# The maxima in the attention heads of a four-layer network: GpSimd subtracts them in every second block, VectorE builds their diagonal matrix

## The chip, the cores and the metric

The kernel runs on one core of a Trainium2 chip. The time is the device time of one execution in microseconds, the median over runs. In the profile TensorE is PE (its weight loads PEld), VectorE is DVE, ScalarE is ACT, GpSimd is POOL, and SyncE, which issues most DMAs, is SP. Everything is float32.

## The reference

Four residual layers act on four images of 32 x 32 pixels with 384 channels. The change lies in layer 0, a deformable attention with six heads of 64 channels:

```python
q = jnp.einsum('bhwc,cd->bhwd', x, w_q) + b_q
...
xs = _bilinear_sample(xg, pos)              # keys and values at learned positions
k = (xs @ w_k + b_k).reshape(Bq, n, HEADS, HC)
v = (xs @ w_v + b_v).reshape(Bq, n, HEADS, HC)
attn = jnp.einsum('bmhc,bnhc->bhmn', qh, k) * scale
bias = _bilinear_sample(rpe_img, disp)      # a bias for each pair of query and key
...
attn = jax.nn.softmax(attn + bias, axis=-1)
out = jnp.einsum('bhmn,bnhc->bmhc', attn, v).reshape(Bq, Hq, Wq, NC)
return out @ w_out + b_out
```

Here n = 1024 pixels, so that each head has 1024 x 1024 logits. Layer 1 is another attention with 12 heads, layer 2 a ratio of box sums, layer 3 a local attention over 3 x 3 windows. A group norm stands before each layer.

## The kernel before, in words

**Front and trunk.** The layer 0 of an image is its front, the layers 1 to 3 are its trunk. The front of image 0 runs alone at the start, through a hand-ordered pipeline of its own (`heads0`, which the diff does not touch). After that the trunk of image b runs together with the front of image b + 1. Both are Python generators that yield weights of their work; `Net.layer3` steps the trunk and, whenever the front has fallen behind its share, the front. Instructions are thus emitted interleaved. The framework then orders each engine's instructions when the program is built, by its own estimates and the dependencies, except where a call pins them. So on the chip each engine has a fixed queue, and a change of one instruction's engine can move others by a few places.

**One half-head** (`head0(h, q)`): one head and half of the queries, 512 of them. There are 12 in an image and 36 in images 1 to 3. Keys lie on the partitions, 128 to a block, in eight blocks j; queries lie along the free axis.

- For each block, GpSimd issues an indirect DMA (L944) that gathers a window of bias rows into `win` (four buffers). ScalarE and VectorE interpolate it in two steps, in `z` (L956, L957) and in `lg` (L961, L962; 13 buffers). TensorE multiplies keys by queries (L968), VectorE adds the product to `lg` (L971) and keeps a running maximum `rmax` (L973, L975).
- Then the maximum over all keys must be had for each query and brought to all partitions. TensorE transposes `rmax` in four squares (L982), VectorE reduces them to `top`, 128 x 4 (L986). GpSimd makes `diag`, four diagonal matrices 128 x 128 with these maxima, out of the identity (L988). TensorE multiplies a matrix of ones by `diag` (L990), so that every partition holds every query's maximum, and ScalarE copies it out of PSUM to `tb`, 128 x 512 (L994).
- Then, block by block, VectorE subtracts `tb` from `lg` in place (L1001), ScalarE takes the exponential in place (L1002), and TensorE adds the block's product with the values to one PSUM bank, `po` (L1003). Each float32 matmul shows as two in the profile. ScalarE copies the result (L1007) and the row of sums (L1016) out.

**What runs beside it.** The trunk's largest stage is layer 1 (`pair`), two heads at a time, eight blocks of keys for each pair. For each block, GpSimd scales the group similarities into `sg` (L1682, two buffers); TensorE makes the logits in `big` (L1699; `big` is a PSUM tile of two banks, with two buffers), ScalarE takes the exponential to `e` (L1707); TensorE makes the group weights out of `sg` (L1729) or by transposing kept ones (L1724), in PSUM `bank` (four buffers); VectorE multiplies `e` by them and sums (L1736); ScalarE keeps a copy for later blocks (L1741); TensorE multiplies by the values (L1671, after VectorE's L1662 to L1665). In between, `sums_step` prepares the next pair: TensorE's scores (L1561) in `big`, VectorE's maxima (L1570), ScalarE's exponentials with sums (L1574). At the end of an image's trunk come layers 2 and 3; there GpSimd adds a tile of 128 x 1024 (L1892).

The methods that the diff touches, and what calls them:

Of the kernel before, what the change touches and what calls it, by code (L numbers as in the profile page):

```python
# [21 lines left out]
ALU = mybir.AluOpType  # L22
# [4 lines left out]
P = 128  # L27
# [39 lines left out]
def bc(ap, axis, n):  # L67

    u = ap.unsqueeze(axis)
    shape = list(u.shape)  # L70
    shape[axis] = n
    return u.broadcast_to(shape)
# [357 lines left out]
class Front(Lane):  # L430
# [500 lines left out]
    def head0(self, h, q):  # L931

        nc, v = self.nc, self.nc.vector
        f = self.f
        k, r0 = h // 2, (h % 2) * GC
        rows = slice(r0, r0 + GC)
        HH, HN = HW // 2, N // 2
        queries = self.qpad[rows, k, 1 + HH * q : 1 + HH * (q + 1), 1 : 1 + HW]
        logits = []
        rmax = self.wt([P, HN], "rmax", 2)  # L940
        for j in range(NJ):
            c = j * G + h
            win = self.wt([P, (HH + 1) * WROW], "win", 4)
            nc.gpsimd.indirect_dma_start(  # L944
                out=win,
                out_offset=None,
                in_=self.strips[:, :],
                in_offset=bass.IndirectOffsetOnAxis(
                    ap=self.widx[:, q, c : c + 1], axis=0
                ),  # L950
            )
            wv = win.rearrange("p (r c) -> p r c", c=WROW)
            sc = lambda i, t: f[:, i, t, c : c + 1]

            z = self.wt([P, HH, HW + 1], "z", 3)
            nc.scalar.activation(z, wv[:, 0:HH, 0 : HW + 1], AF.Copy, scale=sc(1, 1))  # L956
            v.scalar_tensor_tensor(  # L957
                z, wv[:, 1 : HH + 1, 0 : HW + 1], sc(0, 1), z, ALU.mult, ALU.add
            )
            lg = self.wt([P, HH, HW], "lg", 13)  # L960
            nc.scalar.activation(lg, z[:, :, 0:HW], AF.Copy, scale=sc(1, 0))  # L961
            v.scalar_tensor_tensor(lg, z[:, :, 1 : HW + 1], sc(0, 0), lg, ALU.mult, ALU.add)  # L962
            logits.append(lg.rearrange("p y x -> p (y x)"))
            if j % 2:
                ps = [self.bank() for _ in range(2)]
                for u in range(2):
                    w, mov = self.logits_of(h, q, j - 1 + u)
                    nc.tensor.matmul(ps[u], w, mov, start=True, stop=True)  # L968
                for u in range(2):
                    lf = logits[j - 1 + u]  # L970
                    v.tensor_tensor(lf, ps[u], lf, ALU.add)  # L971
                    if j - 1 + u == 1:
                        v.tensor_tensor(rmax, logits[0], lf, ALU.max)  # L973
                    elif j > 1:
                        v.tensor_tensor(rmax, rmax, lf, ALU.max)  # L975
                yield 6


        NI = HN // P
        ps = self.bank()  # L980
        for i in range(NI):
            nc.tensor.transpose(  # L982
                ps[:, i * P : (i + 1) * P], rmax[:, i * P : (i + 1) * P], self.ident
            )
        top = self.wt([P, NI], "top", 2)
        v.tensor_reduce(top, ps.rearrange("p (i n) -> p i n", i=NI), AX.X, ALU.max)  # L986
        diag = self.wt([P, NI, P], "diag", 1)
        nc.gpsimd.tensor_tensor(diag, bc(self.ident, 1, NI), bc(top, 2, P), ALU.mult)  # L988
        ps = self.bank()
        nc.tensor.matmul(  # L990
            ps, self.ones, diag.rearrange("p i n -> p (i n)"), start=True, stop=True
        )
        tb = self.wt([P, HN], "tb", 2)
        nc.scalar.copy(tb, ps)  # L994
        yield 3


        po = self.bank()
        for j in range(NJ):
            lf = logits[j]  # L1000
            v.tensor_tensor(lf, lf, tb, ALU.subtract)  # L1001
            nc.scalar.activation(lf, lf, AF.Exp)  # L1002
            nc.tensor.matmul(po, self.values_of(h, j), lf, start=j == 0, stop=j == NJ - 1)  # L1003
            if j % 2:
                yield 2

        nc.scalar.copy(queries, po[rows, :].rearrange("p (y x) -> p y x", y=HH))  # L1007
        den = self.sums_of(h, po, logits[0])
        nc.sync.dma_start(self.den[h][:, q * HN : (q + 1) * HN], den)
        yield 3  # L1010
# [1142 lines left out]
```

## Time and profile before

| | |
|---|---|
| median of 3 runs | 4373.35 us (4364.13 to 4380.87) |
| the profiled execution | 4344.14 us |
| its span, from the first instruction to the last | 4342.2 us |
| mean granted TensorE clock, as a share of full speed | 0.949 |
| L1001, subtract on VectorE | 288 times, mean 0.689 us |
| L988, diagonal matrix on GpSimd | 36 times, mean 1.085 us |
| L1002, exponential on ScalarE | 288 times, mean 0.625 us |
| L986, reduction on VectorE | 36 times, 0.684 us |

An engine's row in the profile gives its busy time and its share of the span. A group is all instructions of one line, engine and shape; behind the bar stand its busy time, the mean of one, and how long the engine was idle just before these instructions and what ended that. In the order of time a row gives start, duration, engine, line, operation and tiles, and in brackets the idle time before it and its releaser; rows of equal instructions that follow each other are merged, with their number behind the x. The heads of image 1 lie between some 690 and 1460 us of the span, those of images 2 and 3 between some 1770 and 2530, and 2840 and 3600.

### The profile page before, as it was taken

The numbers are of one execution on the slowest core, as the hardware profiler recorded it, in microseconds if no ns is written. First come the engines' busy times: TensorE is split into PE (matmuls) and PEld (weight loads), VectorE is DVE, ScalarE is ACT, GpSimd is POOL, SyncE is SP. The second block draws the span as 40 slices with busy tenths as digits, with TensorE's granted clock in tenths as the row PEclk, the third lists the DMA queues.
The fourth block names the chain that finished last, engine by engine and source line by source line (L and its number), as shares of the span: only waits on it lengthen the run. The fifth ranks groups of instructions, "written<-read, shape, count | busy, mean of one in ns | idle before, by whom it ended". The sixth has DMA issues, their size and how long they took to land.

```text
span 4342.2 us, 45288 instructions
## 1 busy us (share of the span) xinstructions
PE 3921.3 (90%) x14832; PEld 1681.8 (39%) x14832; DVE 3109.8 (72%) x5905; ACT 2304.8 (53%) x3638; POOL 963.9 (22%) x979
## 2 busy tenths in 40 slices
PE   8788989998999898999899989889889999999998
PEld 4333434333334443433333444333333434444444
DVE  4799676878887456787878746578887874566654
ACT  3366344666664334566766423366676642566633
POOL 1754152212121105221212101431121301000000
PEclk9999989998999998999999999899999999999999
DMA  7744353212221455321212154432221214311111
GB/s 161 236 122 118 89 157 106 64 42 81 60 81 40 127 140 147 108 65 46 75 54 81 40 159 143 132 103 60 61 75 47 75 41 134 99 43 26 33 34 44
DMA packets 295397, 385.08 MB, mean 89 GB/s; under 512 B 167858, under 2 KB 228798, under 8 KB 294650
## 3 DMA queue, kind: packets, MB, share of 16 engines
q1 hardware_dynamic: 246336, 217.44, 17.7%
q0 software_dynamic: 39936, 145.53, 11.3%
q10 hardware_dynamic: 8890, 19.23, 1.3%
q8 instruction: 118, 1.93, 0.2%
q14 instruction: 117, 0.96, 0.1%
HBM read 295.63 MB, written 86.75 MB: 88 GB/s over the span
## 4 chain that ended last, share of the span: by engine, by line
PE 49%; DVE 27%; ACT 9%; issue 8%; DMA 4%; POOL 3%; SPq 0%; DVEq 0%; ACTq 0%; POOLq 0%
PE bank L1729 10%; PE big L1699 6%; DVE nmax L1570 4%; PE big L407 4%; PE bank L1003 4%; DVE e L1736 3%; PE bank L421 3%; PE big L1561 3%; ACT big L1574 3%; PE bank L1724 2%; PE bank L1671 2%; PE big L667 2%; DVE z L1122 2%; PE bank L968 2%; DMA win<-strips,widx 2%
## 5 line engine op out<-in xcount | busy, mean ns | idle before, releaser
L1729 PE MATMUL bank<-whole,sg 128*128 128x512 f32 (+3 forms) x2304 | 854.4, 501 | 7.7 <-POOL sg L1682 6.2
L1736 DVE SCALAR_TENSOR_TENSOR e<-bank,gam,e 128x512 f32<-128x512 f32 x768 | 560.4, 747 | 309.9 <-PE bank L1729 189.2
L1574 ACT ACTIVATE big<-big,nmax 128x1024 f32<-128x1024 f32 x384 | 417.5, 1087 | 295.9 <-DVE nmax L1570 294.1
L1729 PEld LDWEIGHTS bank<-whole,sg 128*128 128x128 f32 x2304 | 401.7, 197 | 357.8 <-issue 272.1
L1699 PE MATMUL big<-qa,ka 64*128 64x512 f32 x1536 | 451.6, 669 | 86.7 <-ACT big L1574 82.5
L1570 DVE TENSOR_REDUCE nmax<-big 128x1 f32<-128x1024 f32 x384 | 451.9, 1217 | 62.8 <-PE big L1561 62.8
L1707 ACT ACTIVATE e<-big 128x1024 f32<-128x1024 f32 x384 | 382.1, 1020 | 176.3 <-PE big L1699 166.8
L944 POOL DMA_INDIRECT win<-strips,widx x288 | 314.8, 1093 | 699.8 <-DVE z L957 382.2
L1682 POOL TENSOR_SCALAR sg<-whole,gam 128x512 f32<-128x512 f32 x192 | 149.1, 777 | 1348.1 <-PE bank L1729 1073.0
L1561 PE MATMUL big<-k,q 32*128 32x512 f32 x1536 | 270.2, 670 | 41.6 <-ACT big L1574 30.5
L1699 PEld LDWEIGHTS big<-qa,ka 64*128 64x128 f32 x1536 | 146.9, 197 | 345.1 <-ACT big L1574 177.9
L1003 PE MATMUL bank<-lg,va 128*128 128x512 f32 x576 | 268.2, 607 | 12.9 <-ACT lg L1002 12.9
L751 POOL DMA_INDIRECT gat<-pairs,sidx x192 | 214.6, 1118 | 290.5 <-DVE ix_one L550 233.2
L962 DVE SCALAR_TENSOR_TENSOR lg<-z,bias_f,lg 128x512 f32<-128x512 f32 x288 | 216.3, 768 | 48.9 <-ACT lg L961 47.3
L956 ACT ACTIVATE z<-win,bias_f 128x528 f32<-128x528 f32 x288 | 205.3, 736 | 57.2 <-DVE lg L962 26.2
L1001 DVE TENSOR_TENSOR lg<-lg,tb 128x512 f32<-128x512 f32 x288 | 182.0, 689 | 74.7 <-ACT tb L994 74.7
L957 DVE SCALAR_TENSOR_TENSOR z<-win,bias_f,z 128x528 f32<-128x528 f32 x288 | 214.9, 763 | 20.9 <-ACT z L956 19.0
L1671 PE MATMUL bank<-e,vs 128*32 128x512 f32 x1536 | 210.7, 617 | 17.7 <-DVE vs L1665 17.7
L1741 ACT COPY gn<-bank 128x128 f32<-128x128 f32 (+2 forms) x288 | 106.3, 370 | 209.6 <-DVE e L1736 208.7
L961 ACT ACTIVATE lg<-z,bias_f 128x512 f32<-128x512 f32 x288 | 199.9, 716 | 16.8 <-DVE z L957 13.2
L971 DVE TENSOR_TENSOR lg<-bank,lg 128x512 f32<-128x512 f32 x288 | 191.3, 683 | 12.7 <-PE bank L968 12.0
L968 PE MATMUL bank<-qs,kz 64*128 64x512 f32 x288 | 172.5, 683 | 12.2 <-DVE e L1736 8.5
(326 smaller groups left out, 6315.1 us busy)
## 6 DMA issues: line engine op xcount, KB each, us to landing
q<-qd SPq DMA_DIRECT2D x48, 256.0 KB
xg<-xgd SPq DMA_DIRECT2D x48, 256.0 KB
pairs<-gat SPq DMA_DIRECT2D x48, 192.0 KB
w<-in_gmat SPq DMA_DIRECT2D x15, 576.0 KB
w<-in_Wqkv SPq DMA_DIRECT2D x12, 576.0 KB
a<-in_x SPq DMA_DIRECT2D x16, 384.0 KB
q<-qpad SPq DMA_DIRECT2D x12, 512.0 KB
qs<-q SPq DMA_DIRECT2D x24, 256.0 KB
```

The lines of the kernel that those rows point to most:

```text
L944: nc.gpsimd.indirect_dma_start(out=win, out_offset=None, in_=self.strips[:, :], in_offset=bass.IndirectOffsetOnAxis(ap=self.widx[:, q, c : ...
L962: v.scalar_tensor_tensor(lg, z[:, :, 1 : HW + 1], sc(0, 0), lg, ALU.mult, ALU.add)
L968: nc.tensor.matmul(ps[u], w, mov, start=True, stop=True)
L1003: nc.tensor.matmul(po, self.values_of(h, j), lf, start=j == 0, stop=j == NJ - 1)
L1561: nc.tensor.matmul(ps[r][:, h * 512 : (h + 1) * 512], self.q4[rows, i * P : (i + 1) * P], self.k4[rows, 0:512], start=True, stop=True,)
L1570: top = v.tensor_reduce(nmax[:, r, i : i + 1], ps[r], AX.X, ALU.max, negate=True)
L1574: nc.scalar.activation(ps[r], ps[r], AF.Exp, bias=nmax[:, r, i : i + 1], accum_out=den[:, r, i : i + 1],)
L1671: nc.tensor.matmul(av[r0 : r0 + HD1, :], vs[:, r, :], es[h][:, r, :], start=j == 0, stop=j == NJ - 1,)
L1699: nc.tensor.matmul(ps[:, r, :], ka[rows, j * P : (j + 1) * P], qa[rows, cols], start=True, stop=True,)
L1707: nc.scalar.activation(e, ps, AF.Exp)
L1729: last = nc.tensor.matmul(ps[:, (mid - i0) * P :], sg[:, r, m, :], sim[:, h, r, m, (mid - i0) * P :], start=m == 0, stop=m == 1,)
L1736: v.scalar_tensor_tensor(e[:, r, :], ps, self.gam[:, 1:2], e[:, r, :], ALU.add, ALU.mult, accum_out=tot[:, r, h : h + 1],)
```

## The change

In `head0`, VectorE instead of GpSimd builds `diag`, and GpSimd instead of VectorE subtracts the maxima in the odd blocks, 1, 3, 5 and 7. Nothing else is edited; the line numbers behind L1001 grow by one.

```diff
         diag = self.wt([P, NI, P], "diag", 1)
-        nc.gpsimd.tensor_tensor(diag, bc(self.ident, 1, NI), bc(top, 2, P), ALU.mult)
+        v.tensor_tensor(diag, bc(self.ident, 1, NI), bc(top, 2, P), ALU.mult)
         ps = self.bank()
...
         for j in range(NJ):
             lf = logits[j]
-            v.tensor_tensor(lf, lf, tb, ALU.subtract)
+            eng = nc.gpsimd if j % 2 else v
+            eng.tensor_tensor(lf, lf, tb, ALU.subtract)
             nc.scalar.activation(lf, lf, AF.Exp)
             nc.tensor.matmul(po, self.values_of(h, j), lf, start=j == 0, stop=j == NJ - 1)
```

## The prediction

> **What bounds the kernel now.** I read the page's busy shares and its chain first, then the groups of the lines that the diff touches, then who waits for whom on TensorE, then the instructions in order of time around single half-heads (one head, one half of the queries; 36 of them in images 1 to 3).
>
> Busy shares, and the chain that ended last:
>
> ```profile
> PE 3921.3 (90%) x14832; PEld 1681.8 (39%) x14832; DVE 3109.8 (72%) x5905; ACT 2304.8 (53%) x3638; POOL 963.9 (22%) x979
> ...
> PE 49%; DVE 27%; ACT 9%; issue 8%; DMA 4%; POOL 3%; SPq 0%; DVEq 0%; ACTq 0%; POOLq 0%
> ```
>
> TensorE is the bound and VectorE next: between 690 and 1460 us, where image 1's heads run beside image 0's trunk, TensorE is busy some 91% and VectorE some 80%. So VectorE work taken away pays only where TensorE stands and VectorE is the cause.
>
> The groups concerned (busy us, mean ns, idle before and its cause; first VectorE, then GpSimd):
>
> ```profile
> L1001 DVE TENSOR_TENSOR lg<-lg,tb 128x512 f32<-128x512 f32 x288 | 182.0, 689 | 74.7 <-ACT tb L994 74.7
> ```
>
> ```profile
> L988 POOL TENSOR_TENSOR diag<-ident,top 128x512 f32<-128x512 f32 x36 | 39.1, 1085 | 122.3 <-DVE top L986 110.2 <-DVE rt L1663 12.1
> L1132 POOL TENSOR_TENSOR dg<-ident,bias_f 128x256 f32<-128x256 f32 x48 | 31.7, 661 | 0.9
> L1892 POOL TENSOR_TENSOR whole<-sq,whole 128x1024 f32<-128x1024 f32 x12 | 28.9, 2405 | 205.8 <-ACT sq L1886 205.7
> ```
>
> What TensorE waited for (us in all, times, longest):
>
> ```profile
> PE big L1699 <- ACT big L1574: 82.5, 44, 5.3
> ...
> PE bank L990 <- POOL diag L988: 23.9, 30, 1.3
> ...
> PE bank L1003 <- ACT lg L1002: 12.9, 11, 2.4
> ```
>
> TensorE loses 24 us to the diagonal matrix, 13 us to the exponentials, and most to L1574, which itself waits for VectorE's maxima L1570 (294 us).
>
> One half-head, the second, in order of time:
>
> ```profile
> 826.60 0.68 DVE L986 TENSOR_REDUCE top<-bank 128x4 f32<-128x512 f32 x1
> 827.37 1.04 POOL L988 TENSOR_TENSOR diag<-ident,top 128x512 f32<-128x512 f32 x1 [1.45 <-DVE top L986]
> ...
> 828.46 1.12 PE L990 MATMUL bank<-diag,ones 128*128 128x512 f32 x2 [0.89 <-POOL diag L988]
> ...
> 829.63 0.59 ACT L994 COPY tb<-bank 128x512 f32<-128x512 f32 x1 [0.98 <-PE bank L990]
> 830.25 1.90 DVE L1001 TENSOR_TENSOR lg<-lg,tb 128x512 f32<-128x512 f32 x3 [2.96 <-ACT tb L994]
> ```
>
> Reduction end to tb end is 2.93 us in most half-heads. After T = 830.21 (tb's end) TensorE has no gap for over 10 us: it asks for sums_step's scores (L1561) at 833.33 and for the first exponential (L1003) at 834.39, T + 4.2.
>
> And two meetings of a VectorE and a GpSimd instruction that both read two SBUF tensors (start, us; one half-head each):
>
> ```profile
> 1254.78 1.14 POOL L988 TENSOR_TENSOR diag<-ident,top 128x512 f32<-128x512 f32 x1
> 1254.94 2.19 DVE L962 SCALAR_TENSOR_TENSOR lg<-z,bias_f,lg 128x512 f32<-128x512 f32 x2
> ...
> 1416.66 2.37 POOL L1892 TENSOR_TENSOR whole<-sq,whole 128x1024 f32<-128x1024 f32 x1
> ...
> 1418.46 3.53 DVE L1001 TENSOR_TENSOR lg<-lg,tb 128x512 f32<-128x512 f32 x5 [0.62 <-ACT tb L994]
> ```
>
> Two L962 undisturbed take 1.42 us (780.88); here 2.19, and they end as if the first had begun when GpSimd was done. Five subtracts undisturbed take 3.1 us (eight take 4.91, a pitch of 0.60); here 3.53, as the first waited 0.44 us for GpSimd to end at 1419.03. L988 itself took 1.14 instead of 1.04 behind a VectorE instruction of the same kind.
>
> **The change, part by part.** A price for GpSimd's subtract first; no row shows it. The diagonal matrix, same size, takes 1.04 us undisturbed, but repeats a small operand. L1892 reads two full tensors, as the subtract does: half of 2.40 is 1.20, and with a fixed part of some 0.20 (what 0.62 us for 256 columns and 1.04 for 512 leave) 1.30. Ends 1.04 and 1.30; I take 1.25, near L1892, of which 1.15 in the way of VectorE.
>
> *Diagonal matrix to VectorE.* L986's end to TensorE's start is 1.17 us now (0.08 + 1.04 + 0.05). On VectorE, the next instruction of the same queue in nearly all half-heads, it costs 0.69 (L1001's row; ends 0.60 by pitch, 0.75 as L1736) and some 0.1 of hand-over: 0.38 saved, 0.3 to 0.5. VectorE was idle there (2.96 us before L1001), so its extra 0.69 is covered. TensorE stood at L990 in 30 half-heads, 0.8 us each: 30 x 0.38 = -11 us. What is late next is tb itself, through L990's matmul and the copy.
>
> *Odd subtracts to GpSimd.* VectorE loses 144 x 0.60 = 86 us of subtracts and gains 36 x 0.69 = 25 of diagonal matrices: 61 us free on paper. But even and odd subtracts both read two SBUF tensors and become ready at the same instant. If they take turns, a pair lasts 0.60 + 1.15 = 1.75, eight last 7.0 us instead of 4.91, and VectorE's four end at 5.8 (VectorE first) or 7.0 (GpSimd first): nothing is freed. If a meeting costs only the 0.44 to 0.78 seen above, three meetings cost 1.3 to 2.3 and VectorE's four end at 3.7 to 4.7. I take turns, since both sides show the wait. The Trainium skill (SBUF — State Buffer, "Who interferes with whom") says that a VectorE instruction with two SBUF inputs contends with a GpSimd instruction that reads SBUF, and that whichever is first blocks the other for the whole instruction. By that rule the subtracts would be strictly serial, and the page speaks against this split; the rows above agree for single meetings, and none shows eight in a row.
>
> What covers it, by half-head. In the 2nd, 4th, 6th and 8th (the window above) VectorE does three products L1736 between the subtracts. With turns: three even and two odd subtracts, 3 x 0.60 + 2 x 1.15 = 4.1; two L1736 (1.34) while GpSimd does its third; one subtract and one L1736 (1.27): L1570 starts at T + 6.7, or 7.85 if GpSimd goes first; it started at 837.08, T + 6.87. A wash. The exponentials are in time for TensorE from T + 4.2 on.
>
> *Order of the exponentials.* Built, the changed program has ScalarE do block 1's exponential before block 0's in most half-heads. ScalarE's queue then stands until GpSimd's first subtract is done (T + 1.25 to 1.80), and L1707, which stood at 831.51 and ended T + 2.3, ends at T + 3.4 to 3.9. TensorE's L1561 needs the PSUM that it frees at T + 3.1: it waits 0.3 to 0.8, say 0.5. Four half-heads of an image: 12 x 0.5 = +6 us. In the 11th the first two odd blocks stand ahead of block 0: its exponential starts at T + 4.0 to 4.7 where TensorE asked at T + 2.65: net of the 0.38, +1.3, x 3 = +4.
>
> *The fifth half-head* (reduction at 1001.93) has all four even subtracts ahead of the first L1736, which ran at T + 2.6. With turns they take 6.4 us, L1570 comes some 2.5 us later, and a later L1574 is what TensorE waits 5.10 us for at 1032.11. Bounds 0 and 3.8; 2.5 x 3 = +7.5.
>
> *GpSimd's queue.* Its subtracts wait for tb, 2.9 us longer than the diagonal matrix waited for its maxima, and hold the queue until T + 7. Behind them stand gathers L944 and sg L1682. In 10 of image 1's 12 half-heads the next of these ran at T + 6 or later, most waiting for a free buffer: no cost. In the 5th and 9th one gather ran at T - 1.1 and T + 0.9 and comes some 6 to 8 us later; its z (L956) ran at T + 12 or later and a gather takes 1.0 + 3.9 us to land: nearly covered, 0 to 2 us, counted in the fifth's term. No DMA of SP's moves.
>
> Sum: -11 + 6 + 4 + 7.5 = +6.5 us. The profiled execution took 4344.14 us (span 4342.2 and 1.9 around it), 29 below the median of the runs, 4373.35; I add the sum to the median: 4380. About 0.5%, 22 us, is what a measurement of this kernel can tell from no change.
>
> **The rivals.** *Faster: the two engines overlap.* If GpSimd's subtracts cost VectorE next to nothing, 61 us of VectorE are freed; at VectorE's 27% of the chain that is -16, with -11 for the diagonal matrix and -6 from exponentials that come earlier: -33, so 4340. Against it stand both meetings above; for it, that they are few.
>
> *Slower: the turns reach TensorE.* Eight subtracts take 2.1 us longer (7.0 against 4.91). If this passes through VectorE's L1570 to L1574 and L1699, TensorE's largest wait, in every half-head, it is 36 x 2.1 = +76, less 11: 4438; half of them, 4400. For it: every queue runs in a fixed order, and VectorE was 80% busy. Against: VectorE itself waits 189 us for L1729's products, where lateness is absorbed. It decides where VectorE is over 2 us late when L1570's scores are ready.
>
> *The change does nothing:* excluded; the built order has 4 subtracts in GpSimd's queue in place of each diagonal matrix.
>
> **How the numbers follow.** Within 0.5% (4351 to 4395) 0.42; slower 0.37; faster 0.21. The likeliest case's own range is its bounds, 4351 to 4395. For 8 in 10 it reaches down to the overlap case's 4340 and up past half of the turns reaching TensorE, 4425.
>
> **What would show it.** Right: L1001's rows at over 1 us mean on both engines; VectorE's busy time falling by far less than 61 us; TensorE's wait at L990 down by about 11 us, some new waits of L1561 on L1707; L988 at 0.69 on VectorE. Wrong: VectorE's subtracts still at 0.69 beside GpSimd's (overlap), or L1699's wait for L1574 up by tens of us (slower).

## The result, and the profile after

The changed kernel took 4389.6 us (median of 8 runs, 4382.89 to 4397.98) beside 4365.74 us for the kernel before: ratio 1.0052, 95% interval 1.0039 to 1.0065, or 24 us more. A repetition later gave 1.0069 (1.0047 to 1.0091). Ratios are compared below rather than times, because the kernel before itself took 4337 to 4378 us in the four groups of runs, each of which was timed beside it.

The profiled execution took 4390.47 us. Its busy shares, and the chain that ended last:

```profile
PE 3935.5 (90%) x14832; PEld 1684.0 (38%) x14832; DVE 3160.5 (72%) x5797; ACT 2303.2 (52%) x3638; POOL 1156.0 (26%) x1087
...
PE 46%; DVE 28%; issue 9%; ACT 9%; POOL 4%; DMA 3%; SPq 1%; another core or an unknown queue 0%; DVEq 0%; ACTq 0%; POOLq 0%
```

VectorE has 108 instructions fewer (5797 against 5905) and is busy 51 us longer. The groups say why (busy us, mean ns, idle before and its cause):

```profile
L1002 POOL TENSOR_TENSOR lg<-lg,tb 128x512 f32<-128x512 f32 x144 | 232.9, 1649 | 162.4 <-ACT tb L994 162.3
L1002 DVE TENSOR_TENSOR lg<-lg,tb 128x512 f32<-128x512 f32 x144 | 211.6, 1517 | 48.5 <-ACT tb L994 48.5
...
L988 DVE TENSOR_TENSOR diag<-ident,top 128x512 f32<-128x512 f32 x36 | 24.8, 689 | 0.9
```

A subtract on VectorE went from 0.689 to 1.517 us, and half of the subtracts record 211.6 us where all of them recorded 182.0. What TensorE waited for (us in all, times, longest):

```profile
PE big L1700 <- ACT big L1575: 89.3, 45, 7.0
PE bank L1004 <- ACT lg L1003: 35.6, 18, 2.6
...
PE bank L990 <- DVE diag L988: 15.1, 25, 0.9
```

The wait for the diagonal matrix fell from 23.9 to 15.1 us, the wait for the exponentials rose from 12.9 to 35.6, and the largest wait rose from 82.5 to 89.3. This last rise does not come from the subtracts: the diagonal matrix alone has 89.6 there (below). The second half-head again, in order of time:

```profile
846.53 0.69 DVE L988 TENSOR_TENSOR diag<-ident,top 128x512 f32<-128x512 f32 x1
...
849.12 4.05 DVE L1002 TENSOR_TENSOR lg<-lg,tb 128x512 f32<-128x512 f32 x3 [1.90 <-ACT tb L994]
849.17 6.39 POOL L1002 TENSOR_TENSOR lg<-lg,tb 128x512 f32<-128x512 f32 x4 [4.04 <-ACT tb L994]
...
850.98 1.15 ACT L1003 ACTIVATE lg<-lg 128x512 f32<-128x512 f32 x2 [1.89 <-POOL lg L1002]
852.03 1.00 ACT L1708 ACTIVATE e<-big 128x1024 f32<-128x1024 f32 x1
852.20 2.02 PE L1562 MATMUL big<-k,q 32*128 32x512 f32 x8
...
853.09 0.30 PEld L1562 LDWEIGHTS big<-k,q 32*128 32x128 f32 x6 [0.60 <-ACT e L1708]
...
854.15 5.42 PE L1004 MATMUL bank<-lg,va 128*128 128x512 f32 x12
```

T is 849.09, tb's end. Three subtracts on VectorE last 4.05 us where three lasted 1.90, GpSimd's four 6.39. ScalarE's exponentials stand until GpSimd's first subtract is done, L1708 ends at T + 3.9 instead of T + 2.3, and six of L1562's eight matmuls wait for it: the eight take 2.02 us, and 1.14 where nothing holds them. TensorE's own row shows no wait for that, as it lies inside a busy row; the row of the weight loads (PEld) does. The first product with the values starts at T + 5.1 instead of T + 4.2.

The fifth half-head (rows of several instructions at once; start, us):

```profile
1026.25 7.34 DVE L1002 TENSOR_TENSOR lg<-lg,tb 128x512 f32<-128x512 f32 x4 [0.21 <-ACT tb L994]
1026.89 4.95 POOL L1002 TENSOR_TENSOR lg<-lg,tb 128x512 f32<-128x512 f32 x4
...
1034.18 0.74 DVE L1737 SCALAR_TENSOR_TENSOR e<-bank,gam,e 128x512 f32<-128x512 f32 x1
...
1036.18 2.34 DVE L1571 TENSOR_REDUCE nmax<-big 128x1 f32<-128x1024 f32 x2
```

Here GpSimd's four came back to back and VectorE's four lasted 7.34 us. L1737 starts at T + 8.0 (before: T + 2.6) and L1571 at T + 10.

### The profile page after: what moved, and what is told of

The parts are those of the page before. It is cut to its first block, busy times and chain, and to the rows that moved or that the text cites. A ratio compares the mean times of both kernels' runs of the same rounds, so it can differ in the third digit from the quotient of the medians.

```text
span 4388.7 us, 45357 instructions
## 1 busy us (share of the span) xinstructions
PE 3935.5 (90%) x14832; PEld 1684.0 (38%) x14832; DVE 3160.5 (72%) x5797; ACT 2303.2 (52%) x3638; POOL 1156.0 (26%) x1087
## 4 chain that ended last, share of the span: by engine, by line
PE 46%; DVE 28%; issue 9%; ACT 9%; POOL 4%; DMA 3%; SPq 1%; another core or an unknown queue 0%; DVEq 0%; ACTq 0%; POOLq 0%
PE bank L1730 9%; PE big L1700 6%; PE big L407 4%; DVE nmax L1571 4%; DVE e L1737 4%; PE big L1562 3%; PE bank L421 3%; ACT big L1575 3%; PE bank L1004 3%; POOL gat L751 2%; PE bank L1725 2%; DVE lg L962 2%; DVE lg L1002 2%; PE bank L1672 2%; PE big L1871 2%
## 5 line engine op out<-in xcount | busy, mean ns | idle before, releaser
L1737 DVE SCALAR_TENSOR_TENSOR e<-bank,gam,e 128x512 f32<-128x512 f32 x768 | 560.0, 746 | 309.1 <-PE bank L1730 186.8
L1575 ACT ACTIVATE big<-big,nmax 128x1024 f32<-128x1024 f32 x384 | 417.4, 1087 | 297.0 <-DVE nmax L1571 263.1
L1700 PE MATMUL big<-qa,ka 64*128 64x512 f32 x1536 | 443.7, 670 | 92.9 <-ACT big L1575 89.3
L1571 DVE TENSOR_REDUCE nmax<-big 128x1 f32<-128x1024 f32 x384 | 452.2, 1217 | 65.6 <-PE big L1562 57.0
L1708 ACT ACTIVATE e<-big 128x1024 f32<-128x1024 f32 x384 | 381.7, 1019 | 189.9 <-PE big L1700 169.1
L1562 PE MATMUL big<-k,q 32*128 32x512 f32 x1536 | 282.8, 661 | 41.6 <-issue 22.9
L1004 PE MATMUL bank<-lg,va 128*128 128x512 f32 x576 | 278.1, 624 | 35.6 <-ACT lg L1003 35.6
L1700 PEld LDWEIGHTS big<-qa,ka 64*128 64x128 f32 x1536 | 147.3, 199 | 342.7 <-ACT big L1575 182.2
L1002 POOL TENSOR_TENSOR lg<-lg,tb 128x512 f32<-128x512 f32 x144 | 232.9, 1649 | 162.4 <-ACT tb L994 162.3
L1002 DVE TENSOR_TENSOR lg<-lg,tb 128x512 f32<-128x512 f32 x144 | 211.6, 1517 | 48.5 <-ACT tb L994 48.5
L1003 ACT ACTIVATE lg<-lg 128x512 f32<-128x512 f32 x288 | 165.3, 623 | 84.0 <-POOL lg L1002 60.8
```

The lines of the kernel that those rows point to most:

```text
L1002: eng.tensor_tensor(lf, lf, tb, ALU.subtract)
L1562: nc.tensor.matmul(ps[r][:, h * 512 : (h + 1) * 512], self.q4[rows, i * P : (i + 1) * P], self.k4[rows, 0:512], start=True, stop=True,)
L1571: top = v.tensor_reduce(nmax[:, r, i : i + 1], ps[r], AX.X, ALU.max, negate=True)
L1575: nc.scalar.activation(ps[r], ps[r], AF.Exp, bias=nmax[:, r, i : i + 1], accum_out=den[:, r, i : i + 1],)
L1700: nc.tensor.matmul(ps[:, r, :], ka[rows, j * P : (j + 1) * P], qa[rows, cols], start=True, stop=True,)
L1708: nc.scalar.activation(e, ps, AF.Exp)
```

## The experiments

All ratios are to the kernel before on the same chip.

**The diagonal matrix alone.**

```diff
-        nc.gpsimd.tensor_tensor(diag, bc(self.ident, 1, NI), bc(top, 2, P), ALU.mult)
+        v.tensor_tensor(diag, bc(self.ident, 1, NI), bc(top, 2, P), ALU.mult)
```

> The kernel before with the diagonal matrix on VectorE, all eight subtracts left on VectorE. Theory (the +24 us of the change are a gain at the diagonal matrix and a larger loss at the subtracts): TensorE's wait of 23.9 us at L990 shrinks to some 13, L988 takes 0.69 us on VectorE, reduction end to tb end shortens from 2.93 to 2.55, so 30 x 0.38 = 11 us faster, ratio 0.9975 (0.9965 to 0.9985). Rival (what is saved there turns into a wait behind it, for the copy tb, the bank or VectorE): ratio 0.9990 to 1.0010, and then the subtracts cost only 24 us.

Measured 0.9934 (0.9914 to 0.9954): 29 us faster, more than twice what was expected. The waits at the place are as expected:

```profile
PE big L1699 <- ACT big L1574: 89.6, 46, 5.6
...
PE bank L1003 <- ACT lg L1002: 16.3, 19, 2.4
...
PE bank L990 <- DVE diag L988: 14.8, 24, 0.9
```

**The subtracts alone.**

```diff
-            v.tensor_tensor(lf, lf, tb, ALU.subtract)
+            eng = nc.gpsimd if j % 2 else v
+            eng.tensor_tensor(lf, lf, tb, ALU.subtract)
```

> The kernel before with the odd subtracts on GpSimd, the diagonal matrix left on GpSimd. Theory: the subtracts alone cost 24 + 11 = 35 us, ratio 1.0080 (1.0065 to 1.0095), with both engines' subtracts at 1.5 to 1.7 us as in the changed kernel and TensorE's wait for ScalarE's exponentials at 30 us or more in place of 12.9. Rival (the diagonal matrix gained nothing in the changed kernel): 1.0050, the same as with both edits.

Measured 1.0143 (1.0122 to 1.0164): 62 us slower, also nearly twice what was expected. The means are 1.563 us on VectorE and 1.640 on GpSimd, and TensorE's wait at L1004 is 35.6 us. So the 24 us are the difference of two terms, -29 and about +55, both larger than the prediction had them.

**VectorE's second operand from PSUM.**

```diff
-            eng.tensor_tensor(lf, lf, tb, ALU.subtract)
+            eng.tensor_tensor(lf, lf, tb if j % 2 else ps, ALU.subtract)
```

> The changed kernel, but VectorE's four even subtracts read the maxima from the PSUM bank that L990 filled instead of the copy tb in SBUF, so that they have one SBUF input; GpSimd's four odd ones still read tb. The same instructions on the same engines, and block 1's exponential still queued ahead of block 0's. Theory (VectorE and GpSimd block each other because both read two SBUF tensors): VectorE's subtracts return to some 0.69 us, GpSimd's to 1.25 to 1.3 us, GpSimd's four end at T + 5.1 instead of T + 6.9, the wait of TensorE for the exponentials falls from 35.6 to under 20 us, and VectorE's 61 us are freed: 4335 to 4365, ratio 0.993 to 1.000. Rival (the cost is GpSimd's own: its slower subtract, its queue held from tb to T + 5 with the gathers behind it, and ScalarE's queue standing for it): the durations fall as above, but the time stays over 15 us above the kernel before, ratio 1.0035 to 1.006. If the subtracts stay at 1.5 us or more, reading the same lg tensors' pool, not the second input, is what blocks.

Measured 0.9965 (0.9949 to 0.9981). The two groups (same columns as above):

```profile
L1002 POOL TENSOR_TENSOR lg<-lg,tb 128x512 f32<-128x512 f32 x144 | 179.4, 1280 | 162.0 <-ACT tb L994 161.9
L1002 DVE TENSOR_TENSOR lg<-lg,bank 128x512 f32<-128x512 f32 x144 | 90.9, 682 | 48.6 <-ACT tb L994 48.6
```

Same engines, same instructions, one operand elsewhere: VectorE's subtract falls from 1.517 to 0.682 us, GpSimd's from 1.649 to 1.280, and 38 us of the time come back (1.0052 - 0.9965). So the meeting of two instructions that both read two SBUF tensors is what costs most of the 55. The Trainium skill (SBUF — State Buffer, "Who interferes with whom") says that a VectorE instruction with at most one SBUF input, outside its modes with two ports, does not contend with GpSimd; these rows agree. But against the diagonal matrix alone on the same chip, 0.9934, GpSimd's help shows no gain even without the turns: VectorE is 79 us less busy (3050.0 against 3129.3), and the time is not shorter, rather some 13 us longer, about as much as the intervals can tell. TensorE's wait for the exponentials is still 27.1 us here against 16.3, where under 20 was expected. GpSimd needs 1.28 us for what VectorE does in 0.69, which would explain it; this was not tried by itself.

**The exponentials in the order of the blocks.**

```diff
-            nc.scalar.activation(lf, lf, AF.Exp)
+            self.tc.keep_in_program_order(nc.scalar.activation(lf, lf, AF.Exp))
```

> The changed kernel with ScalarE's exponentials L1003 held in the order of the blocks (0, 1, 2, ...), where the built order has block 1, which waits for GpSimd, ahead of block 0 in most half-heads. Theory (turns): block 0's exponential runs while GpSimd does block 1, so the next e's exponential L1708 ends some 0.6 us earlier in four half-heads of an image: 12 x 0.6 = 7 us, and up to 4 more in the 11th half-head; ratio to the kernel before 1.0025 to 1.004 instead of 1.0052, because blocks 3, 5 and 7 still come at GpSimd's pace. Rival (the order is the main cause of the loss): over 20 us back, ratio 1.0005 or lower. Rival (order does not matter): 1.0045 to 1.006.

Measured 1.0525 (1.0507 to 1.0542), which none expected. Holding these instructions in order moved others too: in the second half-head ScalarE now does the exponential sums L1575, which wait for VectorE's maxima, before block 0's exponential, which starts at T + 11.1. TensorE pays for it (waits, as above):

```profile
PE big L1700 <- ACT big L1575: 128.3, 59, 4.9
PE bank L1004 <- ACT lg L1003: 107.0, 47, 11.0
```

So this run doesn't tell what the order of blocks 0 and 1 alone is worth; that stays open. It does show how much hangs on ScalarE's queue.

**Where the loss lies: the half-heads of one half of the queries at a time.**

```diff
-            eng = nc.gpsimd if j % 2 else v
+            eng = nc.gpsimd if j % 2 and q == 1 else v
```

> The changed kernel with GpSimd's odd subtracts only in the half-heads of the second half of the queries (2nd, 4th, 6th, 8th, 10th, 12th of an image); in the others VectorE does all eight; the diagonal matrix on VectorE everywhere. It places the loss. The prediction had a wash and 12 x 0.5 = +6 us here: 0.9934 + 0.0014 = 0.995. The two traces, changed kernel against diagonal matrix alone, put +1.0, -1.5, +0.8, +1.4 and +1.6 us on the 2nd to 10th, some +10 us for three images: 0.9957 (0.994 to 0.9975). Rival (the loss is spread evenly over the half-heads): half of 53 us, 0.9995.

Measured 0.9975 (0.9962 to 0.9989), at the upper end of what was expected.

```diff
-            eng = nc.gpsimd if j % 2 else v
+            eng = nc.gpsimd if j % 2 and q == 0 else v
```

> The counterpart: GpSimd's odd subtracts only in the half-heads of the first half of the queries (1st, 3rd, 5th, ..., 11th). The prediction had +7.5 us in the 5th and +4 in the 11th: 0.9934 + 0.0026 = 0.996. The traces put +0.4, +1.9, +3.3, +3.1, +1.5 and +1.9 us on the six, some +36 us for three images: 1.0016 (0.9995 to 1.0035). Rival (even): 0.9995.

Measured 1.0022 (1.0010 to 1.0033). Above 0.9934, the two cost 0.0041 and 0.0088, 18 and 38 us: together 56, the subtracts' whole price. (The diagonal matrix alone was timed on another chip; above its repetition's 0.9943, below, they are 14 and 34.) The even split's 0.9995 lies outside both intervals. Two thirds lie in the odd half-heads, of which the prediction had costed two.

**The diagonal matrix twice.**

```diff
         v.tensor_tensor(diag, bc(self.ident, 1, NI), bc(top, 2, P), ALU.mult)
+        v.tensor_tensor(diag, bc(self.ident, 1, NI), bc(top, 2, P), ALU.mult)
```

> The diagonal matrix alone on VectorE, but made twice in a row there, all subtracts on VectorE: 0.60 to 0.69 us more between the reduction and tb, so that tb's end comes 0.2 us later than in the kernel before, while GpSimd's queue stays free of the diagonal matrix. It tells whether the 29 us that the diagonal matrix alone brought came from the path (0.38 us per half-head, and the clock that a longer wait of TensorE lowers) or from elsewhere (GpSimd's queue, the order that was built). Path: ratio 1.000 to 1.005. Elsewhere: 0.994 to 0.997.

Measured 1.0031 (1.0019 to 1.0044): the path. GpSimd's queue is as free as in the run with the diagonal matrix alone, and a later tb costs 0.0097 above 0.9934, some 42 us, or 38 above the repetition's 0.9943 (both of another chip). The plain sum is not 36 x 0.6 = 22, though. tb's end comes 0.73 us later than there in most half-heads, but 2.4 in the eleventh and 1.6 in the twelfth, 33 to 34 us in all 36.

**All eight from PSUM, without the copy tb.**

```diff
-        tb = self.wt([P, HN], "tb", 2)
-        nc.scalar.copy(tb, ps)
...
-            v.tensor_tensor(lf, lf, tb, ALU.subtract)
+            v.tensor_tensor(lf, lf, ps, ALU.subtract)
```

> The diagonal matrix on VectorE, all eight subtracts on VectorE reading the maxima from the PSUM bank that L990 filled; the copy tb (L994) is left out. It shows what holding that bank until the eighth subtract costs or brings, which the run with VectorE's even subtracts from PSUM has in it too. Expected: the first subtract starts some 0.7 us earlier after the reduction (tb's 0.59 and one hand-over), TensorE's 16 us of waits for the exponentials shrink, ratio 0.988 to 0.993. Rival (with four banks, one held 5 to 7 us longer makes TensorE wait for a bank): ratio 0.995 or above, with new waits of TensorE at L968, L1003 or the products for VectorE's subtracts.

> The run with all eight subtracts from the PSUM bank and no copy tb, once more, beside the diagonal matrix alone. If leaving out the copy brings nothing, the two ratios agree within 0.0015; if it brings the 6 us by which TensorE waits less for the exponentials (16.3 against 10.7), this one is lower by 0.0013 or more.

Measured 0.9931 (0.9913 to 0.9949), and 0.9945 (0.9923 to 0.9966) beside the diagonal matrix alone at 0.9943: leaving out the copy brings nothing. The wait for the exponentials did fall, to 10.7 us; where that came back was not found. This version and the diagonal matrix alone both beat the kernels before and after, and neither beats the other.

**Repetitions on one chip, with profiles.**

> The kernel before once more, for a second profile of it on the chip of the three runs beside it. If the first profile of before is typical, image 1's and 2's heads again take some 657 us between their first and last reduction at a granted clock of 0.94 to 0.95, and image 3's 646 at 0.97. If those were single events, all three images come near 646.

> The changed kernel once more. Theory (a gain of some 29 us from the diagonal matrix and a loss of some 53 from the subtracts): 1.004 to 1.0075 beside the kernel before, whatever the chip. If the clock of one chip made the balance, it comes out at 1.010 or more, or below 1.002.

> The diagonal matrix alone on VectorE once more, for its ratio beside the changed kernel and beside the run without tb on one chip. If its 29 us come from the path and the clock, the ratio is again 0.992 to 0.996; if the first chip's clock brought half of them, 0.9965 to 0.998.

The changed kernel had 1.0069, the diagonal matrix alone 0.9943 (0.9925 to 0.9961). The stretches from the first reduction L986 of an image's heads to its last, which hold eleven of its twelve diagonal matrices, for images 1 to 3 (window; us, PE busy, PEld, DVE, ACT, POOL, the granted clock, DMA share, GB/s); first the kernel before, then the diagonal matrix alone, then the changed kernel:

```profile
768.70:1414.13 645.43, 585.09 (x2249) 240.98 (x2250) 527.94 (x1024) 406.94 (x641) 128.63 (x128) 0.97 0.22 62
1830.31:2481.50 651.19, 588.42 (x2249) 242.70 (x2250) 529.18 (x1023) 406.95 (x641) 128.30 (x128) 0.96 0.21 61
2894.06:3540.55 646.49, 584.49 (x2249) 240.96 (x2250) 528.95 (x1023) 407.02 (x641) 127.97 (x128) 0.97 0.22 62
```

```profile
763.54:1404.30 640.76, 583.69 (x2247) 240.06 (x2248) 533.59 (x1034) 407.84 (x641) 119.25 (x117) 0.96 0.22 62
1814.65:2461.12 646.47, 590.70 (x2247) 241.87 (x2248) 533.61 (x1035) 407.67 (x641) 117.37 (x117) 0.95 0.22 62
2870.67:3512.48 641.81, 581.75 (x2247) 240.01 (x2248) 534.21 (x1035) 407.68 (x641) 117.48 (x117) 0.97 0.22 62
```

```profile
762.72:1421.26 658.54, 593.47 (x2247) 243.05 (x2248) 542.87 (x990) 406.51 (x641) 188.12 (x161) 0.96 0.21 61
1834.48:2493.05 658.57, 591.32 (x2247) 242.89 (x2248) 542.02 (x991) 406.86 (x641) 189.84 (x161) 0.96 0.21 61
2905.46:3568.48 663.02, 598.89 (x2247) 244.92 (x2248) 542.68 (x990) 407.06 (x641) 190.69 (x161) 0.95 0.21 60
```

The sums are 1943.1, 1929.0 and 1980.1 us: the diagonal matrix brings 14 here, the subtracts cost 51. In the first profile of before, the same stretches of images 1 and 2 took 656 and 659 us at a clock of 0.95 and 0.94, and image 3's 646 at 0.97, so those two images were single events. One execution can thus have some 19 us more in its heads than another of the same kernel, by TensorE's clock; against the first profile of before the diagonal matrix would bring 33 in these stretches instead of 14. With the matrix made twice they take 1954.0 us (649.1, 653.8 and 651.1), 25 more than with it made once.

## Why the prediction was right, and where it was not

The time was as predicted, 4389.6 against 4380, inside the likeliest case's 4351 to 4395. In part that is luck. The sum of +6.5 us is +24 to +30 beside the kernel before, beyond the 22 us that the case allowed, and was added to a median of three runs, 4373.35, where eight gave 4365.74. The terms are further off than the sum: the subtracts cost 51 to 62 us where it had 17.5, the diagonal matrix brought 25 to 29 by the medians where it had 11, and the two errors have opposite signs.

**Turns: right.** A pair was to last 1.75 us and eight subtracts 7.0; pairs start 1.68 us apart, and eight end 6.9 to 7.0 us after tb in most half-heads. GpSimd's 1.25 us is 1.28 undisturbed. Nothing was freed on VectorE. The rival in which the engines overlap falls with the first two groups.

**Diagonal matrix: the path right, its worth not settled.** Reduction end to tb end fell from 2.93 to 2.53 or 2.59 us in most half-heads, as the 0.38 said, and L990's wait by 9 us instead of 11. It did not fall everywhere: the diagonal matrix is not VectorE's next instruction in the fifth, ninth and eleventh, and in the eleventh the 2.93 became 3.59. On the repetitions' chip tb's end came 10 us earlier over all 36 half-heads.

"30 x 0.38 = -11 us" priced each of these microseconds at one. In the heads' stretches, with one profile each, the 14 us above stand against 9 us of tb, and with the matrix made twice 25 against 29. The medians give more than twice the -11, but not all of that is found there. Of the 30 us between the profiles of the kernel before and of the diagonal matrix alone, 16 lie outside the heads' stretches, 5 of them ahead of the first reduction of image 1, before any edited line has run; and the two profiles of the diagonal matrix alone differ by 26 us outside them. Whether the edit brings anything outside the heads stays open.

TensorE's clock, which the prediction left out, shows in single half-heads. The seventh half-head, from one reduction to the next: the kernel before, the diagonal matrix alone, the changed kernel (columns as above):

```profile
1135.93:1197.87 61.94, 57.53 (x220) 22.47 (x218) 46.81 (x86) 38.46 (x63) 7.24 (x8) 0.97 0.13 34
```

```profile
1130.04:1190.20 60.16, 56.16 (x220) 21.89 (x218) 47.48 (x87) 38.34 (x63) 6.19 (x7) 1.00 0.13 35
```

```profile
1156.00:1163.00 7.00, 6.25 (x13) 2.64 (x14) 0.59 (x1) 5.04 (x8) 0.00 (x0) 0.51 0.17 45
...
1133.64:1197.75 64.11, 58.94 (x220) 23.10 (x218) 48.33 (x84) 38.30 (x63) 13.01 (x11) 0.95 0.12 33
```

The first two wait equally long for L1574 (3.4 us, longest 2.4). The wait at L990 is 0.9 against 0.5 us, yet the half-head is 1.8 us shorter: TensorE is busy 1.4 us less with the same 220 matmuls, at full clock. In the changed kernel the wait for L1575 is 4.6 us (longest 3.6), and behind it the clock is halved for 7 us. Over the heads as a whole it does not explain the difference: the mean clock of these three kernels is alike, and the matrix made twice had 0.97 throughout.

**The costed half-heads: close, one of them by luck.** From one reduction to the next, the changed kernel against the diagonal matrix alone, on one chip, three images summed (worked out from the 36 rows of L986 in each profile): the 2nd, 4th, 6th and 8th half-heads +5.7 us (predicted +6), the fifth +8.3 (+7.5), the eleventh +6.1 (+4). The first pair of profiles gives 5.1, 10.0 and 5.6. The +6 for the order of the exponentials stood as a wait of L1561; it came as L1562's 2.02 us, in all twelve of these half-heads, 12 x 0.88 = 10.6 us. That their sum is still near 6 is luck: the fourth was 2.0 us shorter in the changed kernel, at a clock of 0.96, 0.96 and 0.91 against 0.91 in all three images.

**The step that failed: "The exponentials are in time for TensorE from T + 4.2 on".** It was read from the second half-head, and half-heads of another kind were left out of the sum. The 1st, 3rd, 7th, 9th and 10th cost 4.5, 5.8, 9.0, 8.0 and 3.7 us: 31 of the 51 (1.2, 5.8, 9.2, 4.4 and 4.7 in the first pair of profiles: 25 of 46). In the third TensorE asks much earlier, at T + 0.4. Its waits there, the diagonal matrix alone and the changed kernel:

```profile
PE bank L1003 <- ACT lg L1002: 1.0, 1, 1.0
```

```profile
PE bank L1004 <- ACT lg L1003: 2.6, 1, 2.6
```

Over three images this wait grew from 3.0 to 7.9 us in the first half-head, from 3.0 to 7.9 in the third, from nothing to 3.2 in the fifth, from 1.2 to 5.4 in the tenth and from 1.5 to 4.4 in the eleventh: 20 us together, from 16.0 to 36.0. Of these the prediction had put the first, third and tenth at nothing.

In the seventh it is the rival's mechanism: turns, late maxima L1571 (the second ones start 21.3 us after the reduction's start instead of 20.0), late sums L1575, a longer wait at L1700, and the clock on top. The ninth was not traced to a cause. Over the whole program the rival's path did not carry the loss, though: the wait at L1700 is 88.4 us in the changed kernel's repetition and 89.4 with the diagonal matrix alone. The rival priced every half-head at 2.1 us, 76 in all; the 51 to 62 of the runs come near that, but 20 of the 51 stand as waits for the exponentials and some 11 in L1562's rows.

**GpSimd's queue.** The term of 0 to 2 us for late gathers was not tried by itself. The run with PSUM gives a hint: there GpSimd's queue still waits for tb and does its four subtracts, and image 1 to 3's heads take 1933.6 us (645.5, 645.3 and 642.8), 2 to 5 more than with the diagonal matrix alone (1931.2 and 1929.0). It is no bound, because VectorE's freed time may hide a loss.

## What to carry to other kernels

Before work is moved to a free engine, ask whether both engines read two SBUF tensors at that instant: if so they take turns, and "half of the work moved away" ends later than all of it did on one engine. A single stretch of the trace shows the mechanism but not its price: where a loop's passes stand differently beside the other work, cost every kind of pass. And one profile of each kernel does not price an edit of some 10 us where executions of the same kernel differ by 19 in the stage: set the stage's times from several profiles beside the medians.

## What the runs showed of the hardware

Turns are not always taken. In the fifth half-head above, GpSimd's first subtract began 0.03 us after VectorE's second and did not wait for it: GpSimd did its four in a row, and VectorE's one lasted 5.53 us, until GpSimd's last was done. In the run with the subtracts alone the same happened in the ninth half-head: GpSimd began 0.31 us after VectorE's second, which lasted 5.80 us. In most half-heads GpSimd's first begins 0.05 us after VectorE's first and waits until that is done. What decides between the two was not settled.

A wait of TensorE of 2.4 us may be followed by a lower clock: in the seventh half-head of before it was followed by 4.5 us at a mean of 0.62, and in the run with the diagonal matrix alone a wait of the same 2.4 us was followed by none. The Trainium skill (TensorE: Matmul & The Clock Gate, Part 1, and "HAM oscillation") has a half-rate state, a free-running window of some 3.4 us, and the rule to avoid idle gaps longer than that. The 0.51 over 7 us behind a wait of 3.6 us agrees with the half rate and the rule; the 0.62 behind 2.4 us shows that a gap below 3.4 us doesn't guarantee full clock.
